# Three reorderings in a fused attention and feed-forward kernel: prompt types, row products and key normalization

## The chip, the cores and the metric

The kernel runs on one core of a Trainium2 chip. The metric is the device time of one execution in microseconds (us). Before the change it is 299.06 us, the median of three runs from 297.88 to 299.31 us.

The engines are called as the profile calls them: PE is the matrix engine (PEld its weight loads), DVE the vector engine, ACT the scalar engine that evaluates functions, POOL the GpSimd engine, SP the queue that issues most DMAs.

## The reference

For 64 sequences of 64 tokens with 256 features, two residual layers are computed:

```python
x = x + attn(cond(x, delta_t, amplitudes, frequencies), W_qkv, W_o, log_gamma)
x = x + ffn(cond2(x, W1, b1, v, prompt_type_ids), clip_x, clip_down, w_gate, w_up, w_down)
```

- `cond` rotates pairs of feature halves by an angle: `c = a**delta * cos(f*delta)`, `s = a**delta * sin(f*delta)`, with one `delta` for each sequence and an amplitude and a frequency for each token position.
- `attn` is linear attention with 16 heads of 16 features and a decay `sigmoid(log_gamma)` for each head. Each key is normalized over its 16 features (`rsqrt(var + 1e-5)`). The kernel computes it as masked products: scores of keys and queries, times a table of decays `gam`, times the values.
- `cond2` pools the tokens by a softmax whose mask is a prefix, a suffix, or all but the token itself. Which of the three a sequence has is its prompt type (`itok`, 0, 1 or 2). The result is divided by the number of unmasked tokens.
- `ffn` is a gated feed-forward layer with fake int8 quantization.

## The kernel before, in words

The 4096 tokens are 32 tiles of 128 tokens (two sequences to a tile). Four tiles are a group, and there are eight groups, 0 to 7. After a preparation, the attention and the pooling run in seven steps, `for step in range(1, NG)`. A step treats three groups at once: it projects group `p = step`, does the attention of group `a = step - 1`, and the pooling of group `q = step - 2`. A tail finishes the last groups. Then come the feed-forward products and the output.

The order of instructions on PE, ACT, DVE and POOL is the order in which the program writes them (`manual_schedule`); DMAs go to the SP queue as written. So "ahead of" in the source is "ahead of" on the engine. The planner underneath adds the waits, and decides which buffer a new tile takes over.

Names that matter here:

- `bank(name)` (L150) hands out a bank of PSUM from a pool of four buffers. Nearly every product of PE goes through it: `pk` (keys of `p`, two tiles), `py` (values weighted, two tiles for each half of a group), `pa` and `psr` (scores of the pooling), `pq` (queries, two tiles), `po` (output projection). A tile takes over a buffer when its last reader is done. The products of keys and queries, `psc`, have a pool of their own with four buffers, numbered p = 0 to 3.
- `rows` (L664 to L673) is such a bank. Six small products spread `delta`, frequency and amplitude over 128 partitions; DVE copies the frequency column to `af`, ACT takes the logarithm of the amplitude column (`lna`) and an exponential (`adt`), DVE computes the angles (`ang`, L684). `idle_0(n)` issues n products whose result nobody reads.
- `scale_ys(g)` (L159) is one long POOL instruction for groups above 0; `rotate(g)` (L176) is eight DVE instructions that read its result `ys` and write `xr`. `ys` has one buffer.
- `tf`, `sel`, `cnt` (L790 to L806) are small DVE instructions in the preparation that turn the prompt types `tib` into one-hot selections and counts. They stand behind `rotate(1)`.
- `mask_bias(g)` (L427) is five POOL instructions that make the mask of a group from `sel`.
- `keys(p)` (L234) makes `pk`, squares it on ACT and sums the squares on DVE (`ssq`). `key_root(p)` (L253) is one square root on ACT. `key_norm(p)` (L258) is eight DVE instructions: `var`, a reciprocal, four small ones on `r` (L267 to L270), and two wide ones that read the two `pk` banks and write `kn` (L273).
- `decay(a, r)` (L351) is four DVE instructions (L367) that multiply the four `psc` banks with `gam` and write `at`. `weighted(a, r)` (L370) is 64 products from `at` into the two `py` banks; they go round the four pairs, so that the seventh already needs the last of the four.
- `diagonal(a, r)` (L393) is two ACT and two DVE instructions that write `yT` from `py`; `output(a, r)` (L406) is `po`. `softmax_shift(q)` (L474) begins with a DVE instruction that reads `psr` (L482).

The middle of a step reads:

```python
            keys(p)
            weighted(a, 0)
            diagonal(a, 0)
            scores(a, 1)
            decay(a, 1)
            key_root(p)
            if q >= 0:
                hidden(q)
            key_norm(p)
            queries(p)
            if q >= 0:
                token_scores(q)
                softmax_exp(q)
            output(a, 0)
```

and goes on with `residual(a, 0)`, `weighted(a, 1)`, `diagonal(a, 1)`.

Of the kernel before, what the change touches and what calls it, by code (L numbers as in the profile page):

```python
# [14 lines left out]
AF = mybir.ActivationFunctionType  # L15
ALU = mybir.AluOpType
# [11 lines left out]
def adaln_attn_ffn(  # L28
# [20 lines left out]
    nc = tc.nc  # L49
    B, S, D = x.shape  # L50
    NH = log_gamma.shape[0]
# [5 lines left out]
    NN = NT // P  # L57
# [26 lines left out]
    cs, sel, cnt = c32("cs", 2, NN), c32("sel", 3, NN), c32("cnt", NN)  # L84
# [36 lines left out]
    with ExitStack() as actx:  # L121
# [28 lines left out]
        def bank(name):  # L150
            if spare[0]:
                t = ps_sc.tile([P, 2, 2, 2 * S], F32, tag="sc", name=name)
                return t.rearrange("p i f c -> p (i f c)")
            return ps.tile([P, 512], F32, tag="bank", name=name)
# [4 lines left out]
        def scale_ys(g):  # L159
            if g == 0:  # L160

                ys = pool.tile([P, GT, D], F32, tag="ys", name="ys_0", bufs=1)
                for t in range(GT):
                    nc.scalar.activation(
                        ys[:, t], xg[0][:, t], AF.Copy, scale=cs[:, 1, t : t + 1]
                    )
                T["ys", g] = ys
                return
            tn = slice(g * GT, (g + 1) * GT)
            ys = pool.tile([P, GT, D], F32, tag="ys", name=f"ys_{g}", bufs=1)  # L170
            nc.gpsimd.tensor_tensor(  # L171
                ys, xg[g], cs[:, 1, tn].unsqueeze(2).to_broadcast([P, GT, D]), ALU.mult
            )
            T["ys", g] = ys

        def rotate(g):  # L176

            xs, ys = xg[g], T.pop(("ys", g))
            xr = pool.tile([P, GT, D], F32, tag="xr", name=f"xr_{g}", bufs=1)
            for t in range(GT):  # L180
                c = cs[:, 0, g * GT + t : g * GT + t + 1]
                nc.vector.scalar_tensor_tensor(
                    xr[:, t, 0:P], xs[:, t, 0:P], c, ys[:, t, P:D], ALU.mult, ALU.subtract
                )
                nc.vector.scalar_tensor_tensor(  # L185
                    xr[:, t, P:D], xs[:, t, P:D], c, ys[:, t, 0:P], ALU.mult, ALU.add
                )
            T["xr", g] = xr
# [162 lines left out]
        def decay(g, r, on_pool=()):  # L351
            banks = T.pop(("psc", g, r))
            at = pool.tile([P, 4, 2, 2, 2, S], F32, tag="at", name=f"at_{g}_{r}")
            for p in range(4):
                dst = at[:, p].rearrange("p i f k t -> p i (f k t)")
                scores = banks[p].rearrange("p i f c -> p i (f c)")
                by = (
                    gam[:, p]
                    .rearrange("p f c -> p (f c)")
                    .unsqueeze(1)  # L360
                    .to_broadcast([P, 2, 4 * S])
                )
                if p in on_pool:
                    nc.scalar.copy(dst, scores)
                    nc.gpsimd.tensor_tensor(dst, dst, by, ALU.mult)
                else:
                    nc.vector.tensor_tensor(dst, scores, by, ALU.mult)  # L367
            T["at", g, r] = at
# [80 lines left out]
        def hidden(g, us=both):  # L449

            pu, _ = span(us)
            pa = bank(f"pa_{g}_{us[0]}")[:, 0 : len(us) * P]
            x2v = T.pop(("x2T", g, us)).rearrange("p c (u k l) -> p c k u l", k=2, l=P)
            for kc in range(2):
                for k in range(2):
                    nc.tensor.matmul(
                        pa[k * A : (k + 1) * A, :],
                        w1s[:, kc, :],
                        x2v[:, kc, k, pu],
                        start=(kc == 0),  # L460
                        stop=(kc == 1),
                    )
            th = pool.tile([P, 2 * P], F32, tag="th", name=f"th_{g}_{us[0]}")
            th = th[:, 0 : len(us) * P]
            nc.scalar.activation(th, pa, AF.Tanh, bias=b1s)
            T["th", g, us] = th
# [114 lines left out]
        with tc.tile_pool(name="prep", bufs=1) as prep:  # L581
            V = nc.vector

            def p32(name, *free):
                return prep.tile([P, *free], F32, name=name)

            lgb, af = p32("lgb", NH), p32("af", 1)

            row3 = prep.tile([1, 3, S], F32, name="row3")
            assert B == S  # L590
# [70 lines left out]
            idle_0(5)  # L661


            rows = bank("rows")  # L664
            for k in range(2):
                half = rows[k * S : (k + 1) * S]
                dl = row3[:, 0].rearrange("o (n k) -> o k n", k=2)[:, k]
                for dst, col_of, row_of in (
                    (half[:, 2 : 2 + NN], ones[0:1, 0:S], dl),
                    (half[:, 0:1], row3[:, 1], ones[0:1, 0:1]),  # L670
                    (half[:, 1:2], row3[:, 2], ones[0:1, 0:1]),
                ):
                    nc.tensor.matmul(dst, col_of, row_of, start=True, stop=True)  # L673
            idle_0(7)
            nc.scalar.preload_act_table_set("natural_log_exp_and_others")


            ang, turns, aabs = (p32(n, NN) for n in ("ang", "turns", "aabs"))
            lna, adt, sc = p32("lna", 1), p32("adt", NN), p32("sc", 2, NN)
            dl = rows[:, 2 : 2 + NN]  # L680
            V.tensor_copy(af, rows[:, 0:1])
            nc.scalar.activation(lna, rows[:, 1:2], AF.Ln)
            nc.scalar.activation(adt, dl, AF.Exp, scale=lna)
            V.tensor_scalar_mul(ang, dl, af)  # L684
            V.tensor_scalar(turns, ang, 1.0 / (2.0 * math.pi), MAGIC, ALU.mult, ALU.add)
            V.tensor_scalar_sub(turns, turns, MAGIC)

# [65 lines left out]
            nc.scalar.activation(gexp, gneg, AF.Exp)  # L753
            nc.scalar.activation(gln, gexp, AF.Ln, bias=1.0)


            V.scalar_tensor_tensor(lgam, lgb, 0.0, gln, ALU.min, ALU.subtract)
            for hf in range(2):
# [26 lines left out]
                half = slice(k * A, (k + 1) * A)  # L785
                V.tensor_scalar_mul(vb[half, half], ones[half, half], v1s[half])
            V.tensor_copy(w, pt)
            rotate(1)

            tf = p32("tf", NN)  # L790
            for k in range(2):
                rows = slice(k * S, (k + 1) * S)
                V.tensor_copy(
                    tf[rows].rearrange("p (u k) -> p u k", k=2),
                    tib[rows].rearrange("p (u c k) -> p u c k", c=2, k=2)[:, :, k, :],
                )

            V.tensor_single_scalar(sel[:, 0, :], tf, 0.0, ALU.is_equal)
            V.tensor_single_scalar(sel[:, 1, :], tf, 1.0, ALU.is_equal)
            V.tensor_add(sel[:, 2, :], sel[:, 0, :], sel[:, 1, :])  # L800
            V.tensor_scalar(sel[:, 2, :], sel[:, 2, :], -1.0, 1.0, ALU.mult, ALU.add)
            V.tensor_scalar_mul(cnt, sel[:, 2, :], float(S - 1))
            for k in range(2):
                V.scalar_tensor_tensor(
                    cnt, sel[:, k, :], npre[:, k : k + 1], cnt, ALU.mult, ALU.add
                )  # L806
            scale_ys(2)
            values(0)
            keys_transposed(0)
# [67 lines left out]
        for step in range(1, NG):  # L877
            p, a, q = step, step - 1, step - 2
            scores(a, 0)
            decay(a, 0)  # L880
            if q > 0:
                pooling_out(q - 1)
            T["xT", p] = transposed(T.pop(("xr", p)), p, "xT")
            if q >= 0:
                T["x2T", q, both] = transposed(xg[q], q, "x2T")
            if p + 1 < NG:
                rotate(p + 1)
                if p + 2 < NG:
                    scale_ys(p + 2)

            nc.scalar.preload_act_table_set("sqrt_and_others")
            keys(p)
            weighted(a, 0)
            diagonal(a, 0)
            scores(a, 1)
            decay(a, 1)
            key_root(p)
            if q >= 0:
                hidden(q)
            key_norm(p)  # L900
            queries(p)
            if q >= 0:
                token_scores(q)
                softmax_exp(q)
            output(a, 0)
            residual(a, 0)
            weighted(a, 1)
            diagonal(a, 1)
            if q >= 0:
                softmax_div(q)  # L910
            mask_bias(a)
            if step == 1:

                nc.scalar.activation(csig, clips, AF.Sigmoid)
            if step < 4:
                weight_scale(step - 1)
            values(p)
            keys_transposed(p)
            if step < 4:
                weight_round(step - 1)  # L920
            if q >= 0:
                weights_transposed(q)
            if 2 <= step < 5:
                weight_widen(step - 2)
            output(a, 1)
            residual(a, 1)
            if q >= 0:
                pooling(q)
            if 2 <= step < 4:
                weight_transpose(step - 2)  # L930
# [371 lines left out]
```

## Time and profile before

| | |
|---|---|
| time, median of 3 runs | 299.06 us (297.88 to 299.31) |
| the profiled execution: its own time | 299.68 us |
| its span, first to last instruction | 298.0 us, 8793 instructions |
| granted clock of PE | 0.996 |
| DVE busy | 230.5 us (77%), 496 instructions |
| ACT busy | 198.9 us (67%), 300 instructions |
| POOL busy | 90.0 us (30%), 83 instructions |
| chain that ended last | PE 73%, DVE 18%, ACT 5%, issue 2% |
| preparation | to about 27 us of the span |
| the seven steps | about 27 to 197 us |
| tail of the pooling | 197 to 222 us |
| feed-forward, quantization and output | 222 to 298 us |

The page gives busy times of each engine for one execution. "Idle before" of a group is the time that its engine stood still ahead of those instructions, and behind the arrow stands what ended it. In a timeline a line has its start, its duration, engine, source line, operation, output and inputs. The chain of waits is followed back from the last instruction, at each point to what came last.

### The profile page before, as it was taken

To read this page: it belongs to the slowest core of one execution; us is meant where nothing else is said; L and a number is where in the kernel's file an instruction comes from. 1 tells how busy PE (TensorE), PEld (TensorE's weight loads), DVE (VectorE), ACT (ScalarE), POOL (GpSimd) and SP (SyncE) were. 2 spreads that over 40 slices of the span, in tenths; PEclk is the share of its full clock that TensorE was granted. 3 is DMA by queue.
4 is the path that set the end of the run, shared out by engine and by line. 5 is a ranking of instruction groups with operands and counts; after the bars stand their busy time and mean duration, and the time that the engine had idled before them with its cause. 6 is when DMAs were issued, how large, how long until landed. Compare 5 with 4: busy or idle time off the path is not lost.

```text
span 298.0 us, 8793 instructions
## 1 busy us (share of the span) xinstructions
PE 278.5 (93%) x3794; PEld 200.5 (67%) x3800; DVE 230.5 (77%) x496; ACT 198.9 (67%) x300; POOL 90.0 (30%) x83
## 2 busy tenths in 40 slices
PE   6999899999999999999999999999779999967992
PEld 5977668768858857876885885877534434435881
DVE  6679985887997796698399468556678999986973
ACT  2794558855864864575476466443589999959990
POOL 0232230510150060055001300016114758831592
PEclk9999999999999999999999999999999999999998
DMA  6590621000220220200000000000000000000995
GB/s 201 158 328 34 217 96 46 30 2 11 44 72 0 40 86 0 75 3 3 2 2 0 2 2 2 2 5 2 2 3 0 0 1 2 0 0 2 132 235 199
DMA packets 18061, 15.23 MB, mean 51 GB/s; under 512 B 4966, under 2 KB 17766, under 8 KB 18022
## 3 DMA queue, kind: packets, MB, share of 16 engines
q1 hardware_dynamic: 15906, 12.56, 13.4%
q0 software_dynamic: 2112, 2.10, 4.7%
q8 instruction: 30, 0.49, 0.7%
q14 instruction: 9, 0.07, 0.1%
q10 hardware_dynamic: 4, 0.00, 0.0%
HBM read 7.65 MB, written 6.29 MB: 47 GB/s over the span
## 4 chain that ended last, share of the span: by engine, by line
PE 73%; DVE 18%; ACT 5%; issue 2%; POOL 0%; DVEq 0%; ACTq 0%; POOLq 0%
PE po L411 10%; PE pv L225 9%; PE pk L225 8%; PE pdn L1226 6%; PE py L384 6%; PE pg L1113 5%; PE pq L302 5%; PE pu L1113 5%; PE psc L342 4%; DVE at L367 4%; PE pl L547 3%; PE pxT L212 2%; PE pkT L289 2%; PE idle L659 2%; PE px2T L212 2%
## 5 line engine op out<-in xcount | busy, mean ns | idle before, releaser
L367 DVE TENSOR_TENSOR at<-psc,gam 128x512 f32<-128x512 f32 x62 | 38.5, 682 | 9.0 <-PE psc L342 9.0
L171 POOL TENSOR_TENSOR ys<-x,cs 128x1024 f32<-128x1024 f32 x7 | 13.3, 1893 | 97.4 <-DVE xr L185 79.6
L411 PE MATMUL po<-woT,yT 128*128 128x256 f32 x128 | 30.8, 385 | 0.4 <-DVE kn L273 0.3
L302 PE MATMUL pq<-xT,wqT 128*128 128x512 f32 x64 | 29.5, 604 | 1.0 <-DVE yT L401 1.0
L225 PE MATMUL pv<-wvT,xT 128*128 128x256 f32 x128 | 29.7, 385 | 0.0
L225 PE MATMUL pk<-wkT,xT 128*128 128x256 f32 x128 | 29.1, 380 | 0.2 <-ACT xT L215 0.2
L310 ACT ACTIVATE qbd<-pq,hm 128x512 f32<-128x512 f32 x32 | 20.1, 684 | 12.6 <-PE pq L302 12.6
L411 PEld LDWEIGHTS po<-woT,yT 128*128 128x128 f32 x128 | 23.2, 190 | 5.8 <-DVE kn L273 2.6
L225 PEld LDWEIGHTS pv<-wvT,xT 128*128 128x128 f32 x128 | 23.7, 190 | 4.3 <-issue 1.2
L1142 DVE TENSOR_REDUCE ham<-hT 128x1 f32<-128x1024 f32 (+1 forms) x25 | 25.9, 1083 | 0.1
L225 PEld LDWEIGHTS pk<-wkT,xT 128*128 128x128 f32 x128 | 23.6, 190 | 3.5 <-ACT xT L215 0.7
L1124 ACT ACTIVATE gate<-pg,wsx 128x1024 f32<-128x1024 f32 (+1 forms) x25 | 25.0, 1015 | 1.3 <-PE pg L1113 1.0
L1135 POOL TENSOR_TENSOR hT<-gate,up 128x1024 f32<-128x1024 f32 x10 | 23.5, 2365 | 5.5 <-ACT up L1129 5.5
L1113 PE MATMUL pu<-xq,wuT 128*128 128x512 bf16 (+1 forms) x94 | 22.9, 379 | 1.2 <-DVE hT L1137 1.1
L1113 PE MATMUL pg<-xq,wgT 128*128 128x512 bf16 (+1 forms) x94 | 23.0, 381 | 1.0 <-DVE xq L1049 0.8
L1226 PE MATMUL pdn<-wdT,hq 128*128 128x256 bf16 x192 | 22.0, 273 | 2.0 <-DVE hq L1049 1.9
L1226 PEld LDWEIGHTS <-hq 128*128 128x128 bf16 x192 | 18.3, 98 | 5.9 <-DVE hq L1049 3.8
L302 PEld LDWEIGHTS pq<-xT,wqT 128*128 128x128 f32 x64 | 11.5, 190 | 15.1 <-issue 11.5
L342 PE MATMUL psc<-qbd,kT 32*64 32x128 f32 x1024 | 20.6, 279 | 0.6 <-ACT kT L292 0.3
L400 ACT ACTIVATE yT<-py,hm 128x256 f32<-128x256 f32 x32 | 13.4, 471 | 11.2 <-PE py L384 11.2
L401 DVE SCALAR_TENSOR_TENSOR yT<-py,hm,yT 128x256 f32<-128x256 f32 x32 | 14.0, 479 | 8.3 <-ACT yT L400 8.0
L322 ACT COPY v<-pv 128x512 f32<-128x512 f32 x16 | 9.4, 585 | 16.3 <-PE pv L225 16.3
(201 smaller groups left out, 552.3 us busy)
## 6 DMA issues: line engine op xcount, KB each, us to landing
x<-in_x_dram SPq DMA_DIRECT2D x7, 512.0 KB, 7.4
out_dram<-x SPq DMA_DIRECT2D x4, 512.0 KB, 4.1
out_dram<-x POOLq DMA_DIRECT2D x4, 512.0 KB, 6.8
out_dram<-x SPq DMA_DIRECT2D x7, 256.0 KB, 2.8
wq_nat<-in_L_attn_W_qkv_dram SPq DMA_DIRECT2D x3, 256.0 KB, 4.3
wnat_d<-in_L_ffn_w_down_dram SPq DMA_DIRECT2D x1, 704.0 KB, 7.0
wnat<-in_L_ffn_w_gate_dram SPq DMA_DIRECT2D x1, 640.0 KB
wnat<-in_L_ffn_w_up_dram SPq DMA_DIRECT2D x1, 640.0 KB, 6.7
```

The lines of the kernel that those rows point to most:

```text
L225: nc.tensor.matmul(pk[:, i * D : (i + 1) * D], xT[:, kc, t * P : (t + 1) * P], w[:, kc, :], start=(kc == 0), stop=(kc == 1),)
L302: nc.tensor.matmul(pq, wqT[:, kc, hf * P : (hf + 1) * P], xT[:, kc, :], start=(kc == 0), stop=(kc == 1),)
L310: nc.scalar.activation(qbd[:, hf, :, k, :], pq.rearrange("p (b s) -> p b s", s=S), AF.Copy, scale=hm[:, k : k + 1],)
L342: nc.tensor.matmul(banks[p][k * S : (k + 1) * S, i, hf, :], kT[rows, hf, b * S : (b + 1) * S], qbd[rows, hf, b].rearrange("p k t -> p (k t)"),
L367: nc.vector.tensor_tensor(dst, scores, by, ALU.mult)
L384: nc.tensor.matmul(pys[k][32 * p : 32 * p + 32, i, hf, :], v[half, 2 * r + i, pair * 2 * E : (pair + 1) * 2 * E], at[half, p, i, hf].rearr ...
L411: nc.tensor.matmul(po[:, i * D : (i + 1) * D], yT[:, i, hf].rearrange("p k t -> p (k t)"), woT[:, hf, :], start=(hf == 0), stop=(hf == 1),)
L1113: nc.tensor.matmul(dst[:, k, :] if wide else dst[k * LAST : (k + 1) * LAST, 0, :], w[:, kc, c * P : min((c + 1) * P, FF)], xq[:, kc, g * G ...
L1124: nc.scalar.activation(gates[i], pgu.pop(("g", i)), AF.Silu, scale=wsx[:, 0, c : c + 1])
L1135: nc.gpsimd.tensor_tensor(hs[i], gates.pop(i), ups.pop(i), ALU.mult)
L1142: nc.vector.tensor_reduce(ham[:, i : i + 1], hs.pop(i), AX.XY, ALU.max, apply_absolute_value=True)
L1226: nc.tensor.matmul(pdn[:, i, :], hq[j][:, NF if last else 2 * c + k, tok], wdT[:, c + k if last else c, :], start=(c == 0), stop=(c == NC ...
```

## The change

Three edits. First, the row products go into two banks, one with the frequency (`rows_f`) and one with the amplitude (`rows_a`), each with its own copy of `delta`; the copy to `af` goes, and DVE takes the frequency straight from its bank. Second, the five instructions that make `tf` and the first two selections move ahead of the instruction that makes `lgam` (the logarithm of the decays); the other four (the third selection and `cnt`) move ahead of `rotate(1)`. Third, in each step `key_norm(p)` stands ahead of `decay(a, 1)`.

```diff
-            rows = bank("rows")
-            for k in range(2):
-                half = rows[k * S : (k + 1) * S]
-                dl = row3[:, 0].rearrange("o (n k) -> o k n", k=2)[:, k]
-                for dst, col_of, row_of in (
-                    (half[:, 2 : 2 + NN], ones[0:1, 0:S], dl),
-                    (half[:, 0:1], row3[:, 1], ones[0:1, 0:1]),
-                    (half[:, 1:2], row3[:, 2], ones[0:1, 0:1]),
-                ):
-                    nc.tensor.matmul(dst, col_of, row_of, start=True, stop=True)
+            rows_f, rows_a = bank("rows_f"), bank("rows_a")
+            for i, rows in ((1, rows_f), (2, rows_a)):
+                for k in range(2):
+                    half = rows[k * S : (k + 1) * S]
+                    dl = row3[:, 0].rearrange("o (n k) -> o k n", k=2)[:, k]
+                    for dst, col_of, row_of in (
+                        (half[:, 1 : 1 + NN], ones[0:1, 0:S], dl),
+                        (half[:, 0:1], row3[:, i], ones[0:1, 0:1]),
+                    ):
+                        nc.tensor.matmul(dst, col_of, row_of, start=True, stop=True)
...
-            dl = rows[:, 2 : 2 + NN]
-            V.tensor_copy(af, rows[:, 0:1])
-            nc.scalar.activation(lna, rows[:, 1:2], AF.Ln)
-            nc.scalar.activation(adt, dl, AF.Exp, scale=lna)
-            V.tensor_scalar_mul(ang, dl, af)
+            nc.scalar.activation(lna, rows_a[:, 0:1], AF.Ln)
+            nc.scalar.activation(adt, rows_a[:, 1 : 1 + NN], AF.Exp, scale=lna)
+            V.tensor_scalar_mul(ang, rows_f[:, 1 : 1 + NN], rows_f[:, 0:1])
...
             nc.scalar.activation(gln, gexp, AF.Ln, bias=1.0)
+            tf = p32("tf", NN)
+            for k in range(2):
+                rows = slice(k * S, (k + 1) * S)
+                V.tensor_copy(
+                    tf[rows].rearrange("p (u k) -> p u k", k=2),
+                    tib[rows].rearrange("p (u c k) -> p u c k", c=2, k=2)[:, :, k, :],
+                )
+            V.tensor_single_scalar(sel[:, 0, :], tf, 0.0, ALU.is_equal)
+            V.tensor_single_scalar(sel[:, 1, :], tf, 1.0, ALU.is_equal)
+            V.tensor_add(sel[:, 2, :], sel[:, 0, :], sel[:, 1, :])
...
             V.tensor_copy(w, pt)
-            rotate(1)
...
             V.tensor_scalar(sel[:, 2, :], sel[:, 2, :], -1.0, 1.0, ALU.mult, ALU.add)
             V.tensor_scalar_mul(cnt, sel[:, 2, :], float(S - 1))
             for k in range(2):
                 V.scalar_tensor_tensor(
                     cnt, sel[:, k, :], npre[:, k : k + 1], cnt, ALU.mult, ALU.add
                 )
+            rotate(1)
             scale_ys(2)
...
             scores(a, 1)
-            decay(a, 1)
             key_root(p)
             if q >= 0:
                 hidden(q)
             key_norm(p)
+            decay(a, 1)
             queries(p)
```

More of the change, by code (lines that the diff above doesn't have):

```diff
@@ L585, in p32 @@
                 return prep.tile([P, *free], F32, name=name)
-            lgb, af = p32("lgb", NH), p32("af", 1)
+            lgb = p32("lgb", NH)
             row3 = prep.tile([1, 3, S], F32, name="row3")
@@ L787, in adaln_attn_ffn @@
             V.tensor_copy(w, pt)
-            rotate(1)
[L790 to L800, printed above, removed]
             V.tensor_scalar(sel[:, 2, :], sel[:, 2, :], -1.0, 1.0, ALU.mult, ALU.add)
```

## The prediction

> **What bounds the kernel now.** I read the page first, then the chain of waits, the stretches step by step, the waits, and last the timeline around the three edits. The page and the stretches say that PE fills the steps: step 6 (148.08 to 172.46) has no idle PE at all, step 3 (73.86 to 98.38) 0.06 us in 24.52.
>
> ```profile
> PE 278.5 (93%) x3794; PEld 200.5 (67%) x3800; DVE 230.5 (77%) x496; ACT 198.9 (67%) x300; POOL 90.0 (30%) x83
> ```
> ```profile
> 73.86:98.38 24.52, 24.46 (x421) 18.66 (x423) 20.76 (x46) 16.66 (x30) 5.10 (x6) 1.00 0.16 40
> 148.08:172.46 24.38, 24.38 (x421) 18.65 (x422) 17.95 (x42) 14.37 (x25) 3.43 (x5) 1.00 0.01 2
> ```
>
> So moving DVE work in a step can win little and can lose much. The chain (start, us, what) shows where DVE does come last. In step 3 it leaves PE at `py`, runs through `yT`, the four decays and the key normalization, and returns at `po`; in step 6 it stays on PE.
>
> ```profile
> 80.35 1.14 PE py L384 x64
> 81.50 0.47 ACT yT L400
> 81.99 0.88 DVE yT L401 x2
> 82.86 2.39 DVE at L367 x4
> 85.37 0.47 DVE r L265
> 86.99 0.70 DVE kn L273
> 87.73 1.99 PE po L411 x8
> ...
> 161.46 0.43 PE psr L471 x2
> 161.89 1.92 PE po L411 x8
> ```
>
> Why `kn` holds `po`: they share a bank. The waits (us in total, times, longest) show which tile takes over whose buffer: `psr` that of a query tile, `po` that of a key tile, `py` of the second half that of `psr`, which the softmax's first instruction (`ms`, L482) must have read.
>
> ```profile
> PEld psr L471 <- ACT qbd L310: 2.8, 6, 0.5
> PEld po L411 <- DVE kn L273: 2.6, 6, 0.7
> PEld py L384 <- DVE ms L490: 2.0, 6, 0.3
> ```
>
> **Edit 1, two banks.** Two products are added. Each product is two pieces on PE; the six of before are twelve pieces from 5.24 to 6.27, and the last six take 0.59, so four more cost 0.3 (bounds 0 and 0.4). They lie on the path: the chain runs on PE without a gap from 5.30 through the idle products to `pk` at 13.50, so what follows shifts by 0.3. Gone are `af` (0.16) and the two waits around the shared bank (`lna` starts 0.03 after `af` ends, `ang` idles 0.56 for `adt`): worth nothing, as `xr` from 9.66 lies beside the idle products that run until 9.56; without that cover at most 0.2 back, as the sine would still wait for its table (7.01 to 8.29, sine at 8.63).
>
> **Edit 2, prompt types.** The five instructions (0.35 for two casts, 0.17, 0.17, 0.19: some 1.1 with their spacing) go into a gap of 2.14 on DVE, from 13.79 until `gln` releases `lgam` at 15.93. A POOL instruction runs until 14.19 and may hold them 0.4: they still end by 15.3. If `tib` landed after 14.8, `lgam` would be late by as much; it is issued at 4.74, ahead of group 1's x (5.22), for which POOL started at 12.30. Cost nothing.
>
> The other four (29.45 to 30.35: 0.90) now delay `rotate(1)`, whose `xr` is ready at 27.9 instead of 27.0. PE reads it at 28.20: cover 0.3, and beyond that every 0.1 would cost 0.1. Behind it, `scale_ys(2)` on POOL ends at 29.9 instead of 29.07, `rotate(2)` wants it at 30.6.
>
> What is removed is the worst stall of the preparation: a selection of 0.17 took 1.77 beside a POOL instruction.
>
> ```profile
> 27.18 1.89 POOL L171 TENSOR_TENSOR ys<-x,cs 128x1024 f32<-128x1024 f32 x1 [6.22 <-DVE xr L185]
> 27.35 1.77 DVE L798 TENSOR_SCALAR sel<-tf 128x32 f32<-128x32 f32 x1
> 36.55 3.70 PE L302 MATMUL pq<-xT,wqT 128*128 128x512 f32 x8 [1.02 <-DVE yT L401]
> ```
>
> The first decays so start when their products end, 28.2 instead of 30.35, and all of step 1 on DVE comes 2.1 earlier until `yT`, which then follows ACT: 34.94 instead of 36.03. `pq`'s wait of 1.02 goes. What is late next is in edit 3.
>
> **Edit 3, key normalization first.** In a step without POOL work it costs nothing: from `var` to `kn` it takes 1.69 (159.39 to 161.08), `kn` 1.20 to the next start, the decays 2.48, and the order does not change their sum. DVE starts `var` at 82.78 in step 3; the decays would end at 82.78 + 1.69 + 1.20 + 2.48 = 88.15, while `py` needs them only when `po` is done (89.47). `po` could start when `psr` ends, 87.51 for 87.73: a gain of 0.2 in steps 3 and 4, 0.25 in step 5 (the idle of `po` there).
>
> But in steps 1 to 5 POOL runs `ys` and then five mask instructions in just this stretch: 82.64 to 86.12 in step 3. Before, the decays lay beside them and were not slowed (2.48, as in step 6 with POOL idle: 2.47). The small instructions are slowed, even by the last of the five alone:
>
> ```profile
> 85.40 0.72 POOL L440 TENSOR_TENSOR bias<-bias,biast 128x256 f32<-128x256 f32 x1
> 85.87 0.34 DVE L267 TENSOR_TENSOR r<-r 128x64 f32<-128x64 f32 x1
> ```
> ```profile
> 160.07 0.23 DVE L267 TENSOR_TENSOR r<-r 128x64 f32<-128x64 f32 x1
> ```
>
> The blocked one ended at 86.21, 0.09 after POOL's. The same holds for `var` in step 5 (0.51 for 0.18, 0.06 after POOL's end) and `sel` above. Five instructions can be caught: `var` and the four on `r`; the reciprocal kept 0.54 beside POOL. I let each wait for the running POOL instruction, and POOL's next come between. Step 3: `var` ends 83.31, reciprocal 83.77, then `r` at 84.0, 84.80, 85.48, 86.29, so `kn` starts at 86.33, not 84.47: 1.86 more. The decays end at 86.33 + 3.68 = 90.01; `py` needs the last by its seventh product (0.1 after its start), so it counts as started at 89.93 instead of 89.66: loss 0.27. If DVE wins one of the races, `kn` starts at 85.74 and PE gains 0.19.
>
> The Trainium skill (SBUF — State Buffer, Who interferes with whom) speaks against this edit: a DVE instruction in a two-port mode, or with two inputs in SBUF, and a GpSimd instruction that reads SBUF shut each other out for the whole instruction, whichever comes second waiting. By that rule alone the five waits could take all of the mask work that is left (3.48 us in steps 3 and 4, 2.2 to 2.9 in the others), and the whole change would cost 7.3. By the rows alone (0.12 to 0.33 for a wait, some 1.0 for five) the decays end before `po`, and the change would win 0.3. My walk through the instructions lies between, nearer to the rows.
>
> The other steps, the same way: step 4 has the same offsets, 0.27. In step 2 POOL is further on: `kn` at 61.23 for 60.09, decays end 64.91, ahead of `py` (65.14): 0. Step 5: `kn` 135.57, decays end 139.25, `py` counted 139.2 for 139.37: gain 0.15. Steps 6 and 7: 0. Step 1: `var` at 35.73, POOL's masks from 34.70; `kn` 38.5, decays end 42.2, `py` counted 42.1 for 42.00: loss 0.1, so the 1.02 won by edit 2 is given back here (without blocking `py` could start at 41.05: gain 0.95).
>
> Behind the moved decays on DVE stand the softmax's three, the residual and `yT`; `py` ends that much later too, so they keep their slack (0.90 idle ahead of `yT`).
>
> **Sum** on the profiled execution (299.68 = span 298.0 and 1.68 around it): 0.3 + 0.1 + 0 + 0.27 + 0.27 - 0.15 = 0.8, that is 300.5. The profiled execution is 0.62 above the median; 299.06 + 0.8 = 299.9.
>
> **Rivals.** *Banks stay chained.* The sum lets `psr` take over a key bank, now free earlier, so that `py` no longer waits for `ms`. If the hand-overs stay as the waits show them, `py` also waits for `ms`, which now stands behind the decays: 0.41 more in steps 2 to 5, less slack: 0.3 + 0.1 + 0.1 + 0.68 + 0.68 + 0.25 = 2.1, so 301.2. It decides from the point where the decays end less than 0.41 before `po`, true in steps 2 to 5. Against it: `kn` is free about 2 us earlier than now.
>
> *A query tile takes the key bank.* If the planner expects `kn` before the tanh `th` (83.87 to 84.34, while `kn` unblocked ends at 85.1), the second query tile waits for the blocked `kn`: in step 3 from 85.3 to 87.0, 1.7. In steps 3 and 4 that, in 2 and 5 about 0.9: 5.2, less what is then hidden, with the 0.4 of the start about 5.5: 304.5. This is slower beyond doubt; the 0.8 us between the two ends speak against it.
>
> *POOL yields.* If the small instructions slip between POOL's, edit 2's gain stays: 0.3 - 0.95 - 0.19 - 0.19 - 0.25 = -1.3, and -1.6 if the added products are hidden: 297.5 to 297.8. For it: `var` in steps 3 and 4 lost 0.02 only; against it: that was at POOL's last moments.
>
> **How the numbers follow.** About 0.5%, 1.5 us, is what a measurement can tell from no change: within is 297.6 to 300.6. Forecast 299.9, chance 0.38 (its own range 298.4 to 301.0); chained banks 0.24 at 301.2; the query tile 0.18 at 304.5; POOL yields 0.20 at 297.7. Slower: a tenth of the first, three quarters of the second, all of the third, 0.40. Faster: a twentieth of the first and most of the last, 0.18. The rest, 0.42. The range 297.4 to 304.0 leaves out part of the third and of the last.
>
> **What would show it.** Right: `sel` at 0.17, no wait of `pq` for `yT` in step 1, `var` to `kn` at 2.8 to 3.6 in steps 1 to 5 and 1.69 in 6 and 7, `py` waiting for `at` in steps 1, 3 and 4. Chained banks: `py` waiting for `ms`. Query tile: `pq` waiting for `kn`. Wrong altogether: `var` to `kn` near 1.7 in all steps, or a stall in the preparation, as at `pxT` for `xr`.

## The result, and the profile after

The changed kernel takes 302.85 us (median of four runs, 302.02 to 303.41); the kernel before, on the same chip, 298.78 us (four runs, 297.88 to 299.31). The ratio is 1.0128, with a 95% interval of 1.0106 to 1.0151: slower by 4.1 us, about 1.3%. That is inside the forecast range (297.4 to 304.0), but about 3 us above the number, and it is the result of the rival in which a query tile takes the key bank, not the central case's. The profiled execution took 303.41 us with a span of 301.6 us (before: 298.0).

The page's first line, and the stretches of steps 3 and 6, each from its first `psc` to the next step's. Columns: stretch, its length, then busy time and instructions of PE, PEld, DVE, ACT, POOL, the granted clock, the share of the DMA engines, GB/s.

```profile
PE 279.3 (93%) x3798; PEld 200.8 (67%) x3804; DVE 236.4 (78%) x495; ACT 198.6 (66%) x300; POOL 89.9 (30%) x83
```
```profile
74.20:100.10 25.90, 24.45 (x421) 18.66 (x422) 22.38 (x46) 16.64 (x30) 5.09 (x6) 1.00 0.15 38
152.32:176.50 24.18, 24.18 (x420) 18.70 (x423) 17.94 (x42) 14.37 (x25) 3.44 (x5) 1.00 0.01 2
```

PE has as much work in step 3 as before (24.45 for 24.46), but the step is 25.90 long instead of 24.52: PE now stands still for 1.45. DVE is busy 1.6 longer with the same 46 instructions. Step 6 shows neither and is 0.2 shorter than before.

By the starts of the steps the span's 3.6 us divide so: the preparation is 0.72 shorter, step 1 takes 15.32 instead of 15.09 (counted, here and below, from its second group of `psc`, 7.5 after its first), steps 2 to 5 take 0.83, 1.38, 1.40 and 1.12 more, steps 6 and 7 take 0.20 and 0.21 less, and the rest is 0.23 shorter. Nearly all of the loss, 4.73 us, is in steps 2 to 5. The 0.72 of the preparation goes with a change of PE's speed that the last section shows.

The chain of waits through the middle of step 3 (start, us, what):

```profile
82.33 0.88 DVE yT L401 x2
83.20 0.43 DVE var L261
...
86.57 0.70 DVE kn L273
87.27 0.04 issue
87.31 1.98 PE pq L302 x4
89.30 0.43 PE psr L471 x2
89.73 1.73 PE po L411 x8
```

Before, the chain came back to PE at `po`. Now it comes back at the second `pq`: a query tile waits for the key normalization. The waits of PE say it outright (us in total, times, longest); in the kernel before no `pq` waits for `kn`.

```profile
PEld pq L302 <- DVE kn L273: 9.1, 6, 2.3
PE pq L302 <- DVE kn L273: 4.8, 4, 1.4
```

The 4.8 us over four waits match the 4.73 us of steps 2 to 5. The wait of `pq` for `yT` (1.0 before) is gone from step 1.

Why `kn` is late is seen in the timeline of step 3, the mask instructions of POOL beside the key normalization:

```profile
84.23 0.72 POOL L440 TENSOR_TENSOR bias<-bias,biast 128x256 f32<-128x256 f32 x1
85.04 0.61 POOL L433 TENSOR_TENSOR biast<-cloze,sel 128x256 f32<-128x256 f32 x1
85.73 0.72 POOL L440 TENSOR_TENSOR bias<-bias,biast 128x256 f32<-128x256 f32 x1
```
```profile
84.39 0.65 DVE L268 TENSOR_TENSOR r<-r,var 128x64 f32<-128x64 f32 x1
85.08 0.62 DVE L269 TENSOR_SCALAR r<-r 128x64 f32<-128x64 f32 x1
85.73 0.80 DVE L270 TENSOR_TENSOR r<-r,r 128x64 f32<-128x64 f32 x1
86.57 1.29 DVE L273 TENSOR_TENSOR kn<-pk,r 128x512 f32<-128x512 f32 x2
```

The two engines take turns. POOL's instruction ends at 84.95, 85.65 and 86.45; DVE's small ones end at 85.04, 85.70 and 86.53, each 0.05 to 0.09 later, and POOL's next starts within 0.03 of DVE's end. These three take 0.62 to 0.80 instead of the 0.20 to 0.22 of step 6, where POOL is idle; `var` takes 0.52 for 0.18, and the first instruction on `r` (84.13, 0.23) is not slowed. From `var` to `kn` it is 3.45 us, where a step without POOL takes 1.69.

### The profile page after: what moved, and what is told of

Same layout as the page of the kernel before. It is cut to its first block, busy times and chain, and to the rows that moved or that the text cites. A ratio compares the mean times of both kernels' runs of the same rounds, so it can differ in the third digit from the quotient of the medians.

```text
span 301.6 us, 8806 instructions
## 1 busy us (share of the span) xinstructions
PE 279.3 (93%) x3798; PEld 200.8 (67%) x3804; DVE 236.4 (78%) x495; ACT 198.6 (66%) x300; POOL 89.9 (30%) x83
## 4 chain that ended last, share of the span: by engine, by line
PE 75%; DVE 16%; ACT 5%; issue 2%; POOL 0%; ACTq 0%; DVEq 0%; POOLq 0%
PE pv L225 10%; PE pk L225 9%; PE po L411 9%; PE pq L302 6%; PE py L384 6%; PE pdn L1226 6%; PE pg L1113 5%; PE pu L1113 5%; PE psc L342 4%; PE pl L547 3%; PE pxT L212 2%; PE pkT L289 2%; PE idle L659 2%; PE px2T L212 2%; ACT hq L1045 2%
## 5 line engine op out<-in xcount | busy, mean ns | idle before, releaser
L302 PE MATMUL pq<-xT,wqT 128*128 128x512 f32 x64 | 30.6, 610 | 4.8 <-DVE kn L273 4.8
```

The lines of the kernel that those rows point to most:

```text
L302: nc.tensor.matmul(pq, wqT[:, kc, hf * P : (hf + 1) * P], xT[:, kc, :], start=(kc == 0), stop=(kc == 1),)
```

## The experiments

**Theory A:** two things together make the loss. The planner gives the second query tile the bank of the first key tile, so PE's queries wait for `kn`; and `kn` is late because the five masks on POOL hold the small instructions back. Edit 2 wins about 1.5 by itself. **Rivals:** the early part of the change costs something; the new key order costs whatever bank is used; POOL is not needed for the loss.

**Edits 1 and 2 without the third.**

```diff
+            decay(a, 1)
             key_root(p)
...
             key_norm(p)
-            decay(a, 1)
```

> Edits 1 and 2 alone; the key normalization stays behind the decays. Theory A (edit 3 makes the whole loss): faster than before by 1.5 to 2.0 us: 0.7 from the preparation (the changed kernel's key products start at 12.62 instead of 13.34) and about 1.0 because the first query tile of step 1 no longer waits for yT; steps 2 to 7 keep their lengths of before (24.4 to 24.5 us). Theory B (the added row products or the moved small instructions cost, edit 3 is harmless): not faster than before, and slower if the moved instructions hold up the preparation.

Measured: 297.50 us (296.60 to 298.12) against 299.04, ratio 0.9946 (0.9928 to 0.9963). Step 1 takes 13.85 instead of 15.09; the other steps are as long as before. The early part of the change is a gain of 1.5, and the whole loss lies in the third edit.

**Edit 3 alone.**

> Edit 3 alone, preparation as before. Theory A: slower than before by 5 to 6.5 us: steps 2 to 5 longer by 4.7 together as in the changed kernel, steps 6 and 7 shorter by 0.4, and step 1 longer by 1 to 2, since there the decays of the second half now also end behind the output product and nothing won in the preparation pays for it. Theory B: within 1 us of before.

Measured: 305.34 us (305.00 to 306.35), ratio 1.0217 (1.0190 to 1.0244), 6.3 us slower.

```profile
PE pq L302 <- DVE kn L273: 4.8, 4, 1.5
PE po L411 <- DVE kn L273: 1.0, 1, 1.0
```

The 4.8 are there without the other edits. Step 1 grows by 2.06 to 17.15, since without edit 2 the wait of `pq` for `yT` (1.0) stays and a wait of `po` for `kn` comes on top.

**The whole change, with the second query tile in the bank of `pa`.** The tile is put by hand into the buffer whose reader is the tanh.

```diff
-                pq = bank(f"pq_{g}_{hf}")
+                pq = T.pop("pa") if hf and "pa" in T else bank(f"pq_{g}_{hf}")
```

> The changed kernel, but the second query tile is put by hand into the bank of the pooling's first product (pa), whose tanh is read long before; the blocking by POOL stays. Theory A1 (the bank is what turns a blocked key normalization into a wait of PE): the wait of the queries for kn (4.8 us in the changed kernel) goes; what is left is a wait of the second half's py for the late decays and for ms, 0.1 to 0.8 in each of steps 2 to 5; about 2 us faster than the changed kernel, some 0.5 to 1.5 above before. Theory A2 (late decays cost as much by themselves): as slow as the changed kernel, with py waiting 1.4 in steps 3 and 4.

Measured: 300.54 us (299.40 to 301.58), ratio 1.0054 (1.0032 to 1.0076): 2.3 faster than the change as it is, by the medians of two sessions, and 1.5 slower than before. No `pq` waits for `kn` any more, so the hand-over is the cause of that wait. What is late next is another one:

```profile
PE py L384 <- DVE ms L483: 1.0, 3, 0.4
```

This is the wait of the rival *Banks stay chained*, in a kernel that keeps the second query tile out of the key bank. Steps 3 and 4 take 25.14 each, 0.63 more than before; that rival had priced them at 0.68 each. The late `kn` costs something whichever bank follows it.

**The whole change, with the masks made at the top of the step.** `mask_bias(a)` moves ahead of the step's other work.

> The changed kernel, but the five POOL instructions of each mask are issued at the top of the step, so that from step 2 on they run behind the softmax of the step before, or as soon as their buffer is free, and not beside the key normalization; banks as in the changed kernel. Theory A (POOL blocks the small instructions): var to kn goes from 3.45 to about 1.7 us in steps 2 to 5, the queries no longer wait for kn, steps of 24.2 us as steps 6 and 7 of the changed kernel; 2 us or more faster than before, about 296.8. Theory C (the order on DVE alone is too long, whatever POOL does): steps 2 to 5 stay at 25.2 to 25.9 us, time within 1 us of the changed kernel.

Measured: 298.92 us (297.73 to 300.25, twelve runs), ratio 0.9998 (0.9980 to 1.0017). From step 2 on it goes as expected:

```profile
82.41 0.19 DVE L261 TENSOR_SCALAR var<-ssq 128x64 f32<-128x64 f32 x1
84.10 1.29 DVE L273 TENSOR_TENSOR kn<-pk,r 128x512 f32<-128x512 f32 x2
```

`var` to `kn` is 1.69 again, no PE product waits for `kn`, and the steps take 24.18 (one 24.98). The time was missed by 2.1. The profile shows one reason, step 1: it takes 16.23 instead of 13.85. The masks of groups 0 and 1 now both fall into its stretch. The chain there:

```profile
30.76 0.69 DVE xr L182
31.45 0.81 DVE xr L185
```

`xr` takes 0.69 and 0.81 where it takes 0.26 a little later: the masks of group 0 hold up the rotation of group 2, and those of group 1 the key normalization (`var` to `kn` 3.06, 35.20 to 38.26). The lock was moved, not taken away. Why these twelve runs spread over 2.5 us stays open; the profiled execution was the fastest of them (297.73).

**Masks that wait, decays first in step 1.** The mask tile gets one buffer instead of two, so that a group's masks wait for the softmax of the step (they start at 86.43 in step 3, behind the first read of `psr`). In step 1, where there is no softmax yet, the old order stays.

```diff
-            bias = pool.tile([P, GT, S], F32, tag="bias", name=f"bias_{g}")
+            bias = pool.tile(
+                [P, GT, S], F32, tag="bias" if g < NG - 1 else "bias_z", name=f"bias_{g}", bufs=1
+            )
...
+            if step == 1:
+                decay(a, 1)
...
             key_norm(p)
-            decay(a, 1)
+            if step > 1:
+                decay(a, 1)
```

> The kernel after, with two edits: the tile of the masks has one buffer instead of two, so that each group's mask instructions on POOL wait for the softmax of the step and leave the key normalization alone; and in step 1, where a mask is made beside the key normalization whatever one does, the decays stay ahead of the key normalization as before. Theory A (the query tile loses its time because the key normalization is held back by POOL's mask instructions; without them the new order gains 0.2 us a step by loading the weights of po early): no pq wait for kn, var to kn 1.69 from step 2 on, steps of 24.2 instead of 24.4, so 6 times 0.2 us less than the 297.5 of edits 1 and 2 alone: 296.0 to 296.6. Theory B (the new order costs by itself, POOL only adds to it): above 298. Theory C (step 1's gain in edits 1 and 2 alone came by chance of the preparation and not from the prompt types): 297.2 to 298.0 with step 1 of 15 us.

Measured: 296.58 us (295.95 to 296.90), ratio 0.9907 (0.9891 to 0.9924), faster than both kernels and than theory B allowed. The chain of step 3 is PE alone:

```profile
81.48 3.63 PE pq L302 x8
85.11 0.43 PE psr L473 x2
85.55 1.73 PE po L411 x8
```

The planner still gives the key bank to the query tile (PEld's `pq` still waits for `kn`, at most 0.5), but `kn` is there in time for PE: the eight `pq` run in one piece. `po` takes 1.73 in the chain where it took 1.92 to 1.99 before, because its weights no longer wait for `kn`; that is the 0.2 of a step.

**The control: waiting masks with the old order.**

> The control to the run with waiting masks: edits 1 and 2 with the old key order in every step, and the masks with one buffer. Theory A: masks that wait gain nothing where the decays already lie beside them, so 297.2 to 297.8, as edits 1 and 2 alone (297.5), with steps of 24.4. If the waiting masks by themselves are the gain: 296.0 to 296.6, the same as with the new order.

Measured: 297.09 us (296.38 to 297.54), ratio 0.9925 (0.9907 to 0.9942). Its steps take 24.38. The time is 0.1 below the range expected of theory A: the waiting masks gain a little, since steps 3 and 4 take 24.38 instead of the 24.51 of edits 1 and 2 alone. So most of the gain is not theirs. The new order adds 0.5 us by the medians, where six steps at 0.2 would make 1.2. Six runs each leave the size of this difference open.

**Edit 1 alone, and edit 2 alone.** Each is its own part of the diff and nothing else.

> Edit 1 alone (row products in two banks). Forecast of the prediction: 0.3 us longer, 299.3. Theory A (the four added pieces go in the time in which PE's pieces still run at mixed speed, 16 pieces took 0.97 as 12 did; PE is held by nothing else there): within 0.3 us of before, 298.7 to 299.3. The rival that the missing copy and waits count: 298.3 to 298.8.

Measured: 298.91 us (298.17 to 300.29, twelve runs) against 299.19, ratio 0.9997 (0.9979 to 1.0014). No difference that can be measured; the interval, from 0.6 us faster to 0.4 slower, holds the forecast 0.3 as well as nothing.

> Edit 2 alone (prompt types ahead of lgam and of rotate(1)). Theory A: all of the 1.5 us that edits 1 and 2 won together is edit 2's, through the first decays and the pq wait for yT in step 1 (1.0): 297.4 to 298.0, sel at 0.17, step 1 about 13.9 us instead of 15.1. Rival (edit 1 has half of it): 298.0 to 298.6.

Measured: 298.29 us (297.43 to 298.96, twelve runs), ratio 0.9970 (0.9957 to 0.9983). Step 1 takes 13.85, as with both edits, so its 1.24 are edit 2's alone. The median falls by 0.9, in the rival's range by the number; the rest of the 1.5 is not in the steps, and the intervals of the two runs overlap, so how much of it is edit 1's stays open. In this profile the first `psc` stands at 26.93, with both edits at 25.78. The next runs and the last section show how little that says.

**What belongs to the program, and what to one execution.** The last four are second profiles.

> A second profile of the kernel before, to tell what of the traces belongs to the program and what to the single execution. If the pause of PE within the psc products of step 5 (step 25.2 us instead of 24.4) belongs to the program, it is there again, at the same products; if it comes by chance, step 5 may take 24.4. If the early switch of PE's pieces from slow to fast comes by chance, the first psc of the preparation starts up to 0.7 us away from 26.79.

The kernel before: 298.76 us, span 297.0. The first `psc` is at 25.91 instead of 26.79, and step 5 takes 24.51 instead of 25.20. The program is the same, so both belong to the execution and not to the program.

> A second profile of the kernel after. If what the first showed belongs to the program: pq waits for kn in steps 2 to 5 again (4.8 us in all, 4 times), var to kn 3.4 to 3.5 in steps 3 and 4, steps of 25.2, 25.9, 25.9, 26.3, 24.2 and 24.2. If the interleaving of DVE and POOL comes by chance: other lengths by some tenths, var to kn anywhere from 1.7 to 3.5.

The kernel after: 301.91 us, span 300.2. The mechanism is the same, its size is not:

```profile
PE pq L302 <- DVE kn L273: 3.1, 4, 0.9
```
```profile
85.65 0.22 DVE L270 TENSOR_TENSOR r<-r,r 128x64 f32<-128x64 f32 x1
85.91 1.29 DVE L273 TENSOR_TENSOR kn<-pk,r 128x512 f32<-128x512 f32 x2
```

Here DVE won the last race: POOL's last mask also started at 85.65, and took 0.81 this time, DVE's 0.22. `var` to `kn` is 2.88, and steps 2 to 5 take 25.22, 25.33, 25.33 and 25.35, that is 3.3 more than the second profile of before has, not 4.7.

> A second profile of the kernel with waiting masks and the new order. If the pause in step 5 belongs to the program: a step of 25.0 and five of 24.2 again. If it comes by chance: six steps of 24.2, and a time of 295.3 to 296.

Waiting masks, new order: 295.89 us; six steps of 24.2, the pause gone.

> A second profile of the control in the old order. If its lack of a pause in step 5 belongs to the program: six steps of 24.4 again. If it came by chance: a step of 25.2 in some execution, and the difference between the two orders is 1.2 us where both have the pause or both lack it, 0.2 for each of six steps.

Waiting masks, old order: 297.00 us; a step 5 of 25.05 with the pause, five of 24.38. So the pause visits either kernel, and on the chip of these second profiles as on that of the first two it comes in some and not in others. With the pause in neither, steps 2 to 7 take 145.10 in the new order and 146.26 in the old; with the pause in both, 145.91 and 146.95. The order is worth 1.0 to 1.2 us by the steps.

## Why the prediction was right, and where it was not

The range held; the likeliest case did not come true. The sum put the change at 0.8 us, against 4.1 measured, and the time lies in the range because the range took in part of the query tile's case, which had a chance of 0.18. For the number that is luck; the mechanism of that case had been described. Step by step:

- **Edit 1.** Forecast 0.3 longer; no difference measured, to within half a microsecond. The added pieces are a mis-sized term: in the trace of after, sixteen pieces lie between 5.23 and 6.20, where the idle products start, the same time as twelve before. The 0.59 for the last six was no price for four more.
- **Edit 2, in the preparation.** `sel` at 14.58 took 0.18 and `lgam` started at 15.21, so the gap did hide the five instructions, though the two casts took 1.56 beside POOL rather than 0.35. The stall of 1.77 went, `pq` waits for `yT` no longer, and step 1 shrank by 1.24 for the 1.02 forecast. Right.
- **Edit 3, the lock.** Forecast 3.55 from `var` to `kn` in step 3, measured 3.45, with the engines in turn as walked through. The line on one race won (`kn` 0.6 earlier, so 2.96) is what the second profile shows (2.88). A full lock over all of the masks would have made it 5.2 (1.69 and the 3.48 left of the masks), the bare rows about 2.7 (1.69 and 1.0). The Trainium skill (SBUF — State Buffer, Who interferes with whom) says that two SBUF inputs on DVE and a reading GpSimd instruction contend, and two of the slowed instructions on `r` (L268, L270) agree: 0.65 and 0.80 for 0.22. The third, L269 with 0.62, and `var` read one tensor only; they would come under the two-port mode that the prediction names, but no view shows the mode.
- **Step 1.** Forecast 0.1 longer than before, measured 0.23: the key normalization beside the masks takes back edit 2's gain, now by 1.47 (15.32 for 13.85).
- **Edit 3, the hand-over.** This step failed: "The sum lets `psr` take over a key bank". It was the second query tile that took it. The reason against it was that the tanh ends 0.8 ahead of the unblocked `kn` in the profile. But the planner made the other choice; by which times it decides, the profile of before does not show. The rival's price was about right: 1.7 each for steps 3 and 4 and 0.9 for 2 and 5, 5.2 in all; measured 1.38, 1.40, 0.83 and 1.12, 4.73, and 3.3 where DVE won a race.
- **Steps 6 and 7.** Forecast 0, measured 0.2 less each. The sum had `po` start 0.2 earlier in steps 3 to 5 only; in 6 and 7 its weights, too, had been waiting for `kn`.
- **Chained banks.** Put at 2.1 and not seen in the change, since the longer wait covers it; with the query tile apart it came, at 0.63 of the 0.68 foreseen for step 3. There `psr` does take a key bank, as the sum had it (PEld's `psr` waits for `kn`, 1.4 us in three steps), yet `py` waits for `ms` all the same: that step of the sum fails too.

So the lock's size was read well from a few rows, and its reach was not: 1.8 us of delay costs 0.6 or 1.4 in a step, depending on which tile stands next in line for the bank.

## What to carry to other kernels

When short instructions of DVE are moved, look first at what POOL does at that moment; five of them beside five POOL instructions made the way from `var` to `kn` 1.7 to 2.0 times as long, while four decays in the same place cost nothing. An order that delays a tile's last reader is judged by whoever takes over its bank, and where a planner chooses, each candidate must be priced. It can pay to move the other engine's work instead: one buffer less for the masks, with the old order kept in the one step where that does not help, turned a loss of 1.3% into a gain of 0.9%.

## What the hardware showed beyond that

PE's early products change speed at a time that differs between executions of the same program. The kernel before, first profile and second (timeline):

```profile
9.35 1.91 PE L706 MATMUL pw_wkT<-center,wq_nat 128*128 128x128 f32 x8
11.06 1.06 PE L727 MATMUL pxT<-ident,xr 128*128 128x128 f32 x4
```
```profile
9.35 1.50 PE L706 MATMUL pw_wkT<-center,wq_nat 128*128 128x128 f32 x8
10.69 0.60 PE L727 MATMUL pxT<-ident,xr 128*128 128x128 f32 x4
```

Both start `pw_wkT` at 9.35, with PE busy since 2.80 and these products 0.21 apart. In the first profile the spacing falls to 0.11 at 12.1, in the second at 10.3, and 0.9 us of the difference are left at the first `psc`. The views print a granted clock of 1.00 throughout, but the trace's records of that clock begin only there, at 12.10 and at 10.27, and time without a record is printed as 1.00. In all fourteen profiles the first record, at 9.03 to 12.38, and the change of spacing fall within 0.1 us of each other, and the first `psc`, at 25.48 to 26.93, moves with them. The 0.72 of the preparation go with this (12.10 before, 10.62 after), and so do the 1.15 between the profiles of edit 2 and of both edits (12.38 and 9.99).

The other surprise is the pause of PE among the `psc` of step 5, 0.27 to 0.70 us in eleven of the fourteen profiles, which makes the step about 0.7 to 0.8 us longer where nothing else holds it. The trace names no wait for it. Its DMA records differ, though: in those eleven a packet of 16 KB in the queue of the kind `instruction` starts 1.1 to 1.3 us ahead of the step's first `psc`, in the three without a pause 3.8 us ahead. Whether the later load makes the pause was not tested, and its cause stays open. Speed change and pause together are of the size of the spread between runs, and two profiles of one kernel should be compared step by step before a difference of 0.8 us is given a reason.
